# A subtraction moved from GpSimd to VectorE and behind another instruction, and norm steps moved within attention

## Chip, cores and metric

The kernel runs on one core of one Trainium2 chip. The metric is the device time of one execution in microseconds, the median of several runs. TensorE, VectorE, ScalarE, GpSimd and SyncE each work through a queue of their own in order and wait for one another through semaphores. In profile lines they are PE (PEld for its weight loads), DVE, ACT, POOL and SP; a DMA issued from a queue carries a q, as in SPq.

## The reference, cut to what matters

```python
# x: (8, 512, 32, 32) float32; C = 256, 4 heads of 64, N = 2 blocks
x = x + layer(_gn(x))                       # group norm over 16 channels x 1024 pixels, no affine part

def layer(x):
    t = silu(bn(conv1x1(x, cv1_w)))         # 512 -> 512 channels
    ys = [t[:, :C], t[:, C:]]
    for i in range(N):
        yi = ys[-1]
        z = silu(bn(conv3x3(yi, m_cv1_w[i])))
        q, k, v = conv1x1(z, m_qkv_w[i])    # 256 -> 3 x 256, split in 4 heads
        a = softmax(q^T (k + rw + rh) * 64**-0.5)   # 1024 x 1024 per head
        z = a v
        z = silu(bn(conv1x1(z, m_cv2_w[i])))
        ys.append(yi + z)
    return silu(bn(conv1x1(concat(ys), cv2_w)))     # 1024 -> 512 channels
```

## The kernel before

All data is float32. Images are taken in four pairs (`p` = 0 to 3; image a and image b). For each pair the kernel does, for block n = 0 and then n = 1: a 3x3 convolution of both images together, then for image a and then image b the q/k/v projection and attention, a 1x1 convolution, and the sum with the block's input. In between it does the final 1x1 convolution of the pair (`strassen`), and `cv1` with its group norm for the pair that comes next. The first pair is special in places: its n = 0 projections are direct ones, where all others use Strassen's scheme with seven products.

**The convolution** (`conv3x3`, L610) is Winograd's F(4,3). For each of two output channel blocks (`oc`) it works through i = 0, 1, 2, each with 48 TensorE products into two of three rotating PSUM buffers, and VectorE turns the products back into pixels: `c_t` (L672, L673; they read PSUM and a ScalarE copy `c_m`), `c_e` (L680), `c_r` (L687 to L690), then for i = 0 and 1 `c_k` (L693, L694), at i = 1 two row sets of `z` (L698 to L701) and at i = 2 the other two (L703, L704). ScalarE then applies SiLU in place on `z` (L495), one half image per instruction. For the last channel block at i = 2 the VectorE work is done in two parts (`parts`): first image a's, then image b's.

**The projection** (`project_strassen`, L903) takes `z` as four blocks: channel half times pixel half. It begins with w11 on block b11, then needs t1 = b12 - b11, both in channel block 0. t1 is made by `first_sum` (L897), which writes tile `t_z`. In the seven convolutions that are followed by a Strassen projection (n = 0 of p = 1, 2, 3 and n = 1 of all four) `first_sum` is called inside `conv3x3` at i = 1 of the last channel block (L697), on GpSimd; for image b it is called elsewhere on VectorE. Its products are `p_ps<-t_z,sq` (L916) and `p_ps<-sq,t_z` (L922). ScalarE copies the first products out of PSUM (`u_z`, `m_z`), and later products with z of channel block 1 are added onto the same PSUM buffers. t_z, the two position tables `r_in` (L942, loaded on SyncE's queue) and the kept products share one ring of six buffers (tag `pt`).

**Attention** (`attention_fast`, L1014) runs over four groups g (two heads, half of the queries), each in four steps of two 128-row key blocks. Step (g, at) issues its logits (L1037), ScalarE's exp (L1041), VectorE's accumulation of the denominators (L1055, L1057), and the products with v of the step before (L1071). Where g changes (a border) the finished PSUM buffer is evicted by a ScalarE copy (L1078) and a VectorE addition (L1079), and the next group's products with v wait for it, as there is one such buffer.

**Work behind attention's steps.** The dictionary `behind` hangs small pieces of other work on steps. Key (g, at) or g stands for the step whose v products have just been issued; the piece is queued on its engine behind the accumulation of the step after it. So key (0, 3) is the first border, (1, 3) the second, (2, 3) the third. `NORM_A` (L1964, image a, pairs 1 and 2) and `NORM_B` (L1965, image b, pairs 0 to 2) list the keys at which the generator `group_norm` (L792) for a coming image goes one step on: four statistics of one 128-channel block (L718, L719, VectorE), the mean over a group (`gm_ps`, a TensorE product, L725, and `dev` on VectorE), the reciprocal root (`gv_ps` on TensorE, then VectorE, then GpSimd L745, L802, L803), then the scaling on ScalarE (L809), four whole blocks in A, eight halves in B. In B two of the statistics are done before attention starts.

**What sets the order.** A scheduling layer lays out each engine's queue from the order of the code, a priority and its own idea of readiness; buffers of a ring are given out in the code's order. `tc.issue_after(ins)` puts all that is issued inside it behind `ins` on the same engine.

## Time and profile before

| | |
|---|---|
| runs | 2251.91, 2251.04, 2249.72 us; median 2251.04 |
| the profiled execution's own time | 2249.81 us |
| its span, first to last instruction | 2246.8 us |
| chain that ended last | PE 85%, DVE 11%, the rest 1% or less each |
| granted TensorE clock, mean | 0.999 |
| GpSimd `t_z` | 7 times, 1.28 us each, first at 364.9, last at 1986.4 |
| VectorE `t_z` at the same line (image b) | 7 times, 0.685 us each |
| end of the seven convolutions on TensorE | 372.5, 671.3, 923.0, 1219.6, 1471.0, 1767.3, 1994.0 us |

In a timeline each line is: start in us from the span's start, duration, engine, line and operation, tile written and tiles read, shapes, how often, and in brackets the idle time before it and who ended it. Instructions of VectorE overlap by some tenths of a microsecond, so what one costs the queue is the distance from its start to the next start. "n=1" below means the second block's convolution; the times of the list above alternate n=1, n=0 and so on, the first being n=1 of the first pair.

### The profile page before, as it was taken

To read this page: it belongs to the slowest core of one execution; us is meant where nothing else is said; L and a number is where in the kernel's file an instruction comes from. 1 tells how busy PE (TensorE), PEld (TensorE's weight loads), DVE (VectorE), ACT (ScalarE), POOL (GpSimd) and SP (SyncE) were. 2 spreads that over 40 slices of the span, in tenths; PEclk is the share of its full clock that TensorE was granted. 3 is DMA by queue.
4 is the path that set the end of the run, shared out by engine and by line. 5 is a ranking of instruction groups with operands and counts; after the bars stand their busy time and mean duration, and the time that the engine had idled before them with its cause. 6 is when DMAs were issued, how large, how long until landed. Compare 5 with 4: busy or idle time off the path is not lost.

```text
span 2246.8 us, 40264 instructions
## 1 busy us (share of the span) xinstructions
PE 2200.9 (98%) x16346; PEld 1080.6 (48%) x16346; DVE 1728.7 (77%) x2648; ACT 1099.6 (49%) x1332; POOL 224.4 (10%) x417
## 2 busy tenths in 40 slices
PE   7999999999999999999999999999999999999998
PEld 3653437343474444634447343654344734473443
DVE  7988879878678688877857868986794868797652
ACT  7554653644225665456324666455622455335533
POOL 4322210000220000000021000000012000000001
PEclk9999999999999999999999999999999999999999
DMA  9854447321581324511257141532136611350214
GB/s 273 308 163 150 150 151 261 109 78 45 140 275 49 118 81 145 183 58 67 67 159 261 30 169 35 197 116 77 58 76 173 233 39 34 102 198 30 67 50 112
DMA packets 134309, 285.60 MB, mean 127 GB/s; under 512 B 33540, under 2 KB 61184, under 8 KB 133092
## 3 DMA queue, kind: packets, MB, share of 16 engines
q1 hardware_dynamic: 102212, 197.34, 26.7%
q0 software_dynamic: 31904, 85.61, 13.3%
q8 instruction: 131, 2.15, 0.4%
q14 instruction: 62, 0.51, 0.1%
HBM read 214.86 MB, written 68.03 MB: 126 GB/s over the span
## 4 chain that ended last, share of the span: by engine, by line
PE 85%; DVE 11%; issue 1%; ACT 1%; DMA 1%; SPq 0%; POOL 0%; DVEq 0%; ACTq 0%; POOLq 0%
PE av_ps L1071 18%; PE l_ps L1037 18%; PE c L1305 9%; PE c_ps L653 7%; PE c_new L1305 6%; PE p_ps L916 6%; PE ps L523 5%; PE m_ps L1285 5%; PE x_ps L1405 4%; PE p_ps L922 3%; PE s_ps L1089 1%; DVE acc L1057 1%; DVE c_e L680 1%; PE p_ps L886 1%; DVE c_t L673 1%
## 5 line engine op out<-in xcount | busy, mean ns | idle before, releaser
L1041 ACT ACTIVATE pt<-l_ps 128x1024 f32<-128x1024 f32 x512 | 495.5, 1023 | 332.1 <-PE l_ps L1037 218.8
L1057 DVE TENSOR_TENSOR acc<-acc,pt 128x1024 f32<-128x1024 f32 x384 | 469.6, 1223 | 44.6 <-ACT pt L1041 16.2
L1071 PE MATMUL av_ps<-pt,vT 64*64 64x512 f32 x4096 | 484.8, 590 | 5.2 <-DVE z L1079 4.9
L1037 PE MATMUL l_ps<-q,kr 64*64 64x512 f32 x4096 | 486.3, 590 | 3.0 <-ACT pt L1041 1.9
L1071 PEld LDWEIGHTS av_ps<-pt,vT 64*64 64x64 f32 x4096 | 156.3, 133 | 284.8 <-issue 233.5
L1037 PEld LDWEIGHTS l_ps<-q,kr 64*64 64x64 f32 x4096 | 157.5, 133 | 273.2 <-issue 247.0
L653 PE MATMUL c_ps<-v_in,u 128*64 128x128 f32 x4320 | 239.1, 273 | 2.5 <-issue 2.5
L653 PEld LDWEIGHTS c_ps<-v_in,u 128*64 128x64 f32 x4320 | 235.8, 137 | 9.4 <-issue 9.4
L1285 PE MATMUL m_ps<-z,m_sb 128*128 128x512 f32 x256 | 114.1, 593 | 0.0
L658 ACT COPY c_m<-c_ps 128x512 f32<-128x512 f32 x48 | 28.0, 584 | 170.1 <-PE c_ps L653 140.8
L916 PE MATMUL p_ps<-t_z,sq 128*128 128x512 f32 x224 | 107.0, 595 | 0.0
L1079 DVE TENSOR_TENSOR z<-av_ps,z 128x512 f32<-128x512 f32 x64 | 44.1, 689 | 79.1 <-ACT z L1078 79.1
L1055 DVE TENSOR_TENSOR acc<-pt 128x1024 f32<-128x1024 f32 x64 | 78.0, 1219 | 18.0 <-PE s_ps L1089 11.2
L495 ACT ACTIVATE t<-m_ps,bh,sh 128x512 f32<-128x512 f32 x64 | 46.3, 773 | 91.2 <-PE m_ps L1285 91.2
L916 PE MATMUL p_ps<-z,sq 128*128 128x512 f32 x168 | 80.1, 604 | 5.3 <-ACT z L495 5.2
L1355 POOL DMA_DIRECT2D c_out<-in_x_dram x56 | 50.2, 954 | 293.2 <-ACT c_out L495 288.5
L1285 PEld LDWEIGHTS m_ps<-z,m_sb 128*128 128x128 f32 x256 | 47.8, 190 | 56.8 <-issue 52.5
L1147 DVE TENSOR_TENSOR z<-z,rs 128x512 f32<-128x512 f32 x64 | 42.3, 686 | 27.4 <-DMA rs<-r_dram 27.2
L495 ACT ACTIVATE c_out<-cz,bh,sh 128x512 f32<-128x512 f32 x14 | 16.8, 1301 | 89.1 <-DVE cz L1382 89.1
L495 ACT ACTIVATE z<-z,bh,sh 128x512 f32<-128x512 f32 x64 | 47.6, 804 | 25.8 <-DVE z L704 25.2
L1405 PE MATMUL x_ps<-t_x,sw 128*128 128x512 f32 x128 | 55.9, 592 | 0.0
L922 PEld LDWEIGHTS p_ps<-sq,z 128*128 128x128 f32 x336 | 42.7, 191 | 26.6 <-issue 12.7
(313 smaller groups left out, 3143.4 us busy)
## 6 DMA issues: line engine op xcount, KB each, us to landing
u<-u SPq DMA_DIRECT2D x135, 512.0 KB, 4.8
rs<-r_dram SPq DMA_DIRECT2D x126, 128.0 KB, 3.1
sq<-sq SPq DMA_DIRECT2D x42, 384.0 KB, 5.9
x<-in_x_dram SPq DMA_DIRECT2D x28, 512.0 KB, 7.0
r_in<-r SPq DMA_DIRECT2D x28, 512.0 KB, 4.9
y_in<-y SPq DMA_DIRECT2D x28, 512.0 KB, 4.4
c_out<-in_x_dram POOLq DMA_DIRECT2D x56, 256.0 KB, 5.1
out_dram<-c_out POOLq DMA_DIRECT2D x56, 256.0 KB, 3.3
```

What stands on the lines that cost most here:

```text
L495: silued[0] = nc.scalar.activation(dst, src, AF.Silu, scale=sh[:, k : k + 1], bias=bh[:, k : k + 1])
L523: last_product[0] = nc.tensor.matmul(ps[:, half, :], w_of(k), rhs_of(k, half), start=(k == begin), stop=(k == end))
L653: conv_product[0] = nc.tensor.matmul(to[o], us[cp][:, k, row, c, o], rhs, start=(k == 0), stop=(k == NM - 1),)
L916: nc.tensor.matmul(ps[:, o, :], w[:, o, :], rhs, start=not onto, stop=True, skip_group_check=onto)
L922: nc.tensor.matmul(v[:, ts(j, P)], rhs[:, ts(j, P)], w[:, 2, :], start=j == 0 and not onto, stop=True, skip_group_check=True,)
L1037: nc.tensor.matmul(ps[kh * HD : (kh + 1) * HD, hd, :], kr[r, c, o : o + HD], q[r, c, ts(half, HALF)], start=True, stop=True,)
L1041: last_exp[0] = exp = nc.scalar.activation(pt, ps, AF.Exp, scale=SCALE)
L1057: ins = nc.vector.tensor_tensor(accs[g], accs[g], pt[i], ALU.add)
L1071: nc.tensor.matmul(avs[g][hd * HD : (hd + 1) * HD, kh, :], vT[r, j, o : o + HD], pt[i][r, hd, :], start=(j == 0), stop=(j == NJ - 1),)
L1285: nc.tensor.matmul(pss[half][:, oc, :], m2_sb[:, n, k, ts(oc, P)], ao[:, k, ts(half, HALF)], start=(k == 0), stop=(k == NM - 1),)
L1305: nc.tensor.matmul(ps[:, o, :], w[:, k, ts(o, P)], rhs[part][:, c], start=(k == 0 and not onto), stop=(k == KB - 1), skip_group_check=onto,)
L1405: nc.tensor.matmul(ps[:, o, :], w[:, c, ts(o, P)], rhs[c], start=(c == 0 and not onto), stop=(c == 1), skip_group_check=onto,)
```

## The change

The call of `first_sum` in `conv3x3` moves from i = 1 to i = 2, and from GpSimd to VectorE: it is issued behind image a's last `z` instruction (L704, the new `placed`), ahead of image b's part. `first_sum` loses its engine argument. `NORM_A` has key 1 in place of (2, 3), and `NORM_B` has key 1 in place of (0, 1); as each key moves the same generator by one step, the steps between shift with it.

```diff
                         if i == 1:
-                            if oc == NM - 1 and summed is not None:
-                                t = first_sum(summed, nc.gpsimd)
                             stt(dst[:, 1], tiles(big_d), -0.5, tiles(d_), ALU.mult, ALU.add)
...
                         if final:
                             stt(dst[:, 0, tl], tiles(r0), -6.0, tiles(big_s[:, xs_]), ALU.mult, ALU.add)
-                            stt(dst[:, 3, tl], tiles(r1), -6.0, tiles(big_d[:, xs_]), ALU.mult, ALU.add)
+                            placed = stt(dst[:, 3, tl], tiles(r1), -6.0, tiles(big_d[:, xs_]), ALU.mult, ALU.add)
+                            if oc == NM - 1 and part == 0 and summed is not None:
+                                with tc.issue_after(placed.ins):
+                                    t = first_sum(summed)
...
-        def first_sum(z, engine=nc.vector):
+        def first_sum(z):
             t = act.tile([P, 2, HALF], F32, tag="pt", name="t_z", bufs=n_pt)
-            engine.tensor_tensor(t[:, 0], z[:, 0, ts(1, HALF)], z[:, 0, ts(0, HALF)], ALU.subtract)
+            nc.vector.tensor_tensor(t[:, 0], z[:, 0, ts(1, HALF)], z[:, 0, ts(0, HALF)], ALU.subtract)
...
-        NORM_A = ((0, 1), (0, 3), (1, 1), (1, 2), 2, (2, 1), (2, 2), (2, 3), 3, (3, 1))
-        NORM_B = ((0, 1), (0, 3), (1, 1), (1, 2), 2, (2, 1), (2, 2), (2, 3), 3, (3, 1), (3, 2), (3, 3))
+        NORM_A = ((0, 1), (0, 3), 1, (1, 1), (1, 2), 2, (2, 1), (2, 2), 3, (3, 1))
+        NORM_B = ((0, 3), 1, (1, 1), (1, 2), 2, (2, 1), (2, 2), (2, 3), 3, (3, 1), (3, 2), (3, 3))
```

In the changed program the queues stand so at each of the seven handovers. VectorE has t_z between image a's L704 and image b's L687. TensorE has the 128x128 products with z ahead of the products with t_z, where they stood behind the first of them. ScalarE has two SiLU instructions of image a, then `u_z`, two more, then `m_z`, where `u_z` and `m_z` stood ahead of all four. On SyncE's queue the two `r_in` loads stand behind later weight loads of the ring. In image a's attention of pairs 1 and 2 the `gm_ps` product stands one step ahead of the second border, where it stood behind it.

## The prediction

> **What bounds the kernel now.** I read the page's first part, then what TensorE waits for, then the timelines around one convolution's end and one attention.

> ```profile
> PE 2200.9 (98%) x16346; PEld 1080.6 (48%) x16346; DVE 1728.7 (77%) x2648; ACT 1099.6 (49%) x1332; POOL 224.4 (10%) x417
> ```

> ```profile
> PE p_ps L916 <- ACT z L495: 5.2, 6, 0.9
> PE av_ps L1071 <- DVE z L1079: 4.9, 5, 1.6
> ...
> PE p_ps L922 <- DVE c_t L673: 2.5, 4, 0.6
> ```

> (columns: total us, times, longest). TensorE is busy all but 45.9 us of the span, in one queue, in order. So a microsecond that TensorE waits anywhere is a microsecond of the span, unless a later wait shrinks by it, and later waits are few. The change can win at most the waits shown: 5.2 + 2.5 where seven convolutions hand over to the projection, and 4.6 of the 4.9 at borders that its norm steps touch (1.57 at 739.08 and 1287.38, 0.90 at 818.49, 0.55 at 1366.43).

> The handover, TensorE (start, duration, line):

> ```profile
> 372.47 1.98 PE L916 MATMUL p_ps<-z,sq 128*128 128x512 f32 x4
> 374.29 1.88 PE L916 MATMUL p_ps<-t_z,sq 128*128 128x512 f32 x4
> 376.80 1.13 PE L922 MATMUL p_ps<-sq,z 128*128 128x128 f32 x8 [0.63 <-DVE c_t L673]
> 377.76 1.06 PE L922 MATMUL p_ps<-sq,t_z 128*128 128x128 f32 x8
> 379.69 3.70 PE L916 MATMUL p_ps<-z,sq 128*128 128x512 f32 x8 [0.87 <-ACT z L495]
> ```

> VectorE and GpSimd at the same place:

> ```profile
> 364.70 0.69 DVE L680 SCALAR_TENSOR_TENSOR c_e<-c_ps,c_t 128x512 f32<-128x512 f32 x1
> 365.30 1.15 DVE L688 SCALAR_TENSOR_TENSOR c_r<-c_t 128x256 f32<-128x256 f32 x1
> ...
> 376.24 0.42 DVE L673 TENSOR_TENSOR c_t<-c_ps,c_m 128x256 f32<-128x256 f32 x1
> ...
> 378.37 0.42 DVE L704 SCALAR_TENSOR_TENSOR z<-c_r,c_k 128x256 f32<-128x256 f32 x1
> 378.71 0.28 DVE L687 SCALAR_TENSOR_TENSOR c_r<-c_t,c_e 128x128 f32<-128x128 f32 x1
> ```

> ```profile
> 364.89 1.28 POOL L900 TENSOR_TENSOR t_z<-z 128x512 f32<-128x512 f32 x1 [19.18 <-ACT z L495]
> ```

> VectorE runs without a gap from 365 to 382, behind TensorE. GpSimd's t_z (1.28 us) lies over it and L688 takes 1.15 in place of 0.42. But t_z is ready at 366.2, eight microseconds before TensorE reads it at 374.29.

> **Part 1, the difference on VectorE.** Removed: seven GpSimd t_z, and what they cost VectorE. By the start-to-start distances L688 lasts 1.08 where 0.33 is usual: 0.75 lost, in the four convolutions n=1 (372, 923, 1471, 1994). In n=0 of the second and third pair (671, 1219) L687 loses 1.71 - 0.33 = 1.38. In n=0 of the last pair (1767) nothing: the t_z of 1761.06 lies over L672 and L673, which read PSUM and keep their 0.68. Sum 4 x 0.75 + 2 x 1.38 = 5.8 us. [...]

> Added: a VectorE subtraction of 0.68 (0.60 start to start; the same line already runs seven times on VectorE with median 0.685), placed behind L704 of the first image's part in the changed program's order. That is late: TensorE's s1 products need t_z. The changed program also has TensorE's order moved: z products (1.82), then the four 128x128 z products (0.96), then t_z's. Worked out for the handover at 372.47: VectorE is 0.75 earlier, so L673 ends at 376.66 - 0.75 = 375.91, and the 128x128 products start 0.14 later at 376.05 (as 376.80 stood to 376.66) and are through at 377.0. L704 starts at 377.62, t_z at 377.96, ends 378.64; TensorE gets it at 378.76, a wait of 1.75. Then 1.81 for s1 on t_z, 0.96 for its 128x128 products: the next z products start at 381.53, where they started at 379.69. **+1.84 us**, four times.

> At 671.32: t_z runs 675.48 to 676.16, TensorE has it at 676.28, z products at 679.06 instead of 677.84: **+1.22**, twice. At 1767.31 nothing is won: L704 at 1771.15, t_z until 1772.17, z products at 1775.07 instead of 1772.83: **+2.24**, once. Sum 7.36 + 2.44 + 2.24 = **+12.0 us**. From 379.69 to the first logits at 393.10 TensorE has no idle, so the delay goes straight on.

> What else moves: ScalarE's u_z copy falls behind two of the first image's z activations and m_z behind all four. In the sum ScalarE does activations 378.07 to 379.6, u_z to 380.6, two more to 382.1, m_z to 383.1; TensorE wants u_z gone at 381.5 and m_z at 383.3. This just fits, 0.2 us spare: 0, or up to 0.5 a handover (+3.5). Not below 0. On SyncE's queue the two r_in loads fall behind up to six ring loads, the last of which waits for the convolution's last product: issue near 373.5 instead of 362.84, landing 3.5 to 6.0 (the page's table of DMA issues has 4.9), so by 379.6; VectorE's L946 asks for it at 383.42 + 1.8. Cost 0. On GpSimd's queue the stores behind t_z can only start earlier: 0.

> **Part 2, norm steps.** In the first image's attention (second and third pair of images) statistics three and four, the reciprocal root and the first two activations go one step earlier (a step is two 128-row blocks, some 3.43 us of TensorE), the second activation thereby off border three; the mean goes two steps earlier. In the second image's attention (first to third pair) statistic three goes two steps later, onto border one, and statistic four one step later, off it.

> ```profile
> 717.06 1.90 PE L1037 MATMUL l_ps<-q,kr 64*64 64x512 f32 x16
> ...
> 725.09 0.17 PE L725 MATMUL gm_ps<-mv,gmat 64*64 64x4 f32 x1
> ...
> 739.08 1.95 PE L1071 MATMUL av_ps<-pt,vT 64*64 64x512 f32 x16 [1.57 <-DVE z L1079]
> ```

> ```profile
> 719.53 1.28 DVE L718 BATCH_NORM_STATS2 st<-x 128x6 f32<-128x512 f32 x2
> 720.84 0.21 DVE L719 BATCH_NORM_AGGREGATE mv<-st 128x2 f32<-128x12 f32 x1
> ```

> gm_ps is a TensorE product in the same queue. It now stands 4.2 us behind its last statistic. In the changed order it stands two pairs of steps earlier, at 717.06, but its last statistic only one: VectorE needs from 711.87 one accumulation (1.13), statistics (1.31 and 0.13), two accumulations (2.42), statistics (1.31 and 0.21): 718.38. TensorE stands still until 718.5: +1.44. Later exp(2,3) is behind the moved activation, exp(3,0) and the border's copy end about 738.4, its VectorE half at 739.1, and the border's products start at 739.15 in place of 739.08. So what the border gives (1.1 to 1.2 of the 1.57, after the shift) the gm_ps wait takes: **+0.1**, twice.

> Second image: the border at 818.49 is met with 0.05 wait instead of 0.90, but gm_ps then stands at 822.85 with its statistic at 823.6: wait 0.9, net +0.1. At 1366.43: 0.55 won, 0.9 paid, **+0.4**. First pair (263): no border wait to win; statistic four and a u step end at 270.4 where gm_ps stood at 269.20, then gv_ps 274.6 for 273.20: **+1.4**. Sum of part 2: **+2.0 us**; its ends are -4.6 (all border waits gone, no new one) and +4.

> The new waits could cost more than their length: [...] The longest new wait is 1.8 us. The row nearest is the 1.57 us wait at 739.08, whose 16 products take 1.95 against 1.90 before. By the row 0[...]. I take 0 and leave it for the far tail.

> Together +12.0 + 2.0 = **+14.0 us** on the profiled execution: 2249.8 + 14.0 = 2263.8 (its span 2246.8, and 3.0 around it, unchanged). The median of the runs shown is 2251.04, 1.2 higher, within their spread of 2.2; I say 2264.

> **Rivals.** (A) The norm steps give what they cost before and gm_ps does not wait: +12.0 - 4.6 = +7.4, 2257. For it: the order of VectorE's queue is known, my start times of the statistics are not measured. Against: VectorE's queue is full there. (B) ScalarE is late: m_z misses its 0.2 us spare, +14 + 3.5, 2267. For it: seven activations and copies end to end; against: all durations are rows. (C) The other side: VectorE, not TensorE, sets the pace after the handover. Its last convolution instruction comes 0.15 earlier four times, 0.78 earlier twice, 0.60 later once: -1.6, and with the borders' -4.6 it is -6.2, 2243.6. It decides if TensorE has slack of 1.8 us between handover and attention. For it: VectorE runs 17 instructions into the attention (to 397.9). Against: VectorE idles there 1.08, 2.99 and 0.79 for ScalarE and TensorE, and TensorE never for it. (D) The subtraction isn't late at all: excluded, the changed order has it behind L704, and the products read it.

> **Chances.** My forecast (2260 to 2266) 0.65, A 0.12, B 0.13, C 0.05, rest (half clock, or waits absorbed to within noise) 0.05. Range 2256 to 2269 takes in A, B and the forecast. About 0.2%, 4.5 us, is what a measurement tells from no change. Slower 0.92, same 0.03, faster 0.05.

> **What would show it.** Right: TensorE's wait for DVE t_z of about 1.75 us before L917's t_z products in seven places (none for ScalarE's z any more), gm_ps waits near 1 us for L720 in five attentions, L688 back at 0.42. Wrong: z products less than 7.5 us behind a convolution's last product; or border waits gone without gm_ps waits (A); or waits for ScalarE u_z or m_z (B).

## The result and the profile after

The changed kernel's six runs have a median of 2266.12 us (2263.44 to 2268.74), those of the kernel before beside them 2250.76 us (2249.72 to 2253.74): ratio 1.0066, 95% interval 1.0053 to 1.0079. It is slower by 15.4 us. The execution that was profiled is its slowest, 2268.74 us with a span of 2267.4, against 2249.81 us for the profiled one of before.

Part 1 of the page, and below it TensorE's waits (total us, times, longest), both of the changed kernel:

```profile
PE 2209.2 (97%) x16346; PEld 1087.7 (48%) x16346; DVE 1727.0 (76%) x2655; ACT 1098.7 (48%) x1332; POOL 215.1 (9%) x410
```

```profile
PE gm_ps L726 <- DVE mv L720: 13.3, 6, 7.9
PE p_ps L917 <- DVE t_z L901: 10.6, 7, 1.5
PE p_ps L923 <- DVE c_t L673: 7.3, 7, 1.6
...
PE av_ps L1072 <- DVE z L1080: 0.3, 1, 0.3
```

The waits are where the sum put them: a new one for t_z at all seven handovers; c_t's grown from 2.5 us to 7.3; the one for ScalarE's z (5.2) gone; border waits from 4.9 to 0.3; and five new gm_ps waits (13.3 less the start's 7.9). But TensorE's busy time has also grown, by 8.3 us, with the same number of products. The sum had put nothing there. (Line numbers from L696 on differ by one or two from those of before.)

TensorE's timeline of the changed kernel at the first handover (n=1), and at the next (n=0, where c_t had been waited for only 0.28 us):

```profile
377.69 1.13 PE L923 MATMUL p_ps<-sq,z 128*128 128x128 f32 x8 [1.61 <-DVE c_t L673]
380.34 3.78 PE L917 MATMUL p_ps<-t_z,sq 128*128 128x512 f32 x4 [1.52 <-DVE t_z L901]
...
682.41 1.98 PE L917 MATMUL p_ps<-t_z,sq 128*128 128x512 f32 x4 [1.52 <-DVE t_z L901]
```

Four products on t_z take 1.98 us at 682.41 and 3.78 at 380.34. The busy times of one stretch name the reason (start:end and length; busy time and instructions of PE, PEld, DVE, ACT and POOL; granted TensorE clock; DMA share; GB/s):

```profile
380.30:385.00 4.70, 4.66 (x10) 2.60 (x11) 3.36 (x9) 4.10 (x6) 0.00 (x0) 0.50 0.07 27
```

TensorE came out of two idle stretches, 1.61 and 1.52 us with 1.1 us of work between, at half clock (0.50 granted), and the four products took 3.78 us in place of 1.98. In this execution that happened at 380, 936 and 1489, but not at 2017 after the very same two waits.

On VectorE the sum's picture holds:

```profile
366.93 0.41 DVE L688 SCALAR_TENSOR_TENSOR c_r<-c_t 128x256 f32<-128x256 f32 x1
...
379.60 0.69 DVE L901 TENSOR_TENSOR t_z<-z 128x512 f32<-128x512 f32 x1
```

L688 is back at 0.41 (1.15 before). t_z ends at 380.29, and TensorE starts on it 0.05 us later. VectorE's next instruction starts at 380.20: the overlap that start-to-start distances take off is 0.08 or 0.09 us here, not some tenths.

### The profile page after: what moved, and what is told of

It is laid out like the page before. It is cut to its first block, busy times and chain, and to the rows that moved or that the text cites. A ratio compares the mean times of both kernels' runs of the same rounds, so it can differ in the third digit from the quotient of the medians.

```text
span 2267.4 us, 40245 instructions
## 1 busy us (share of the span) xinstructions
PE 2209.2 (97%) x16346; PEld 1087.7 (48%) x16346; DVE 1727.0 (76%) x2655; ACT 1098.7 (48%) x1332; POOL 215.1 (9%) x410
## 4 chain that ended last, share of the span: by engine, by line
PE 85%; DVE 11%; issue 1%; ACT 1%; POOL 0%; DVEq 0%; ACTq 0%
PE av_ps L1072 18%; PE l_ps L1038 18%; PE c L1306 9%; PE p_ps L917 7%; PE c_ps L653 6%; PE c_new L1306 6%; PE ps L523 5%; PE m_ps L1286 5%; PE x_ps L1406 4%; PE p_ps L923 3%; PE s_ps L1090 1%; DVE acc L1058 1%; DVE c_e L680 1%; DVE c_t L673 1%; PE p_ps L887 1%
## 5 line engine op out<-in xcount | busy, mean ns | idle before, releaser
L917 PE MATMUL p_ps<-t_z,sq 128*128 128x512 f32 x224 | 111.6, 622 | 10.6 <-DVE t_z L901 10.6
L1056 DVE TENSOR_TENSOR acc<-pt 128x1024 f32<-128x1024 f32 x64 | 78.0, 1218 | 18.0 <-PE s_ps L1090 11.2
L495 ACT ACTIVATE t<-m_ps,bh,sh 128x512 f32<-128x512 f32 x64 | 46.3, 774 | 91.0 <-PE m_ps L1286 91.0
L917 PE MATMUL p_ps<-z,sq 128*128 128x512 f32 x168 | 81.0, 603 | 0.0
L495 ACT ACTIVATE z<-z,bh,sh 128x512 f32<-128x512 f32 x64 | 47.7, 805 | 59.5 <-DVE z L702 59.4
L917 PEld LDWEIGHTS p_ps<-t_z,sq 128*128 128x128 f32 x224 | 40.4, 198 | 46.8 <-issue 32.7
L495 ACT ACTIVATE c_out<-cz,bh,sh 128x512 f32<-128x512 f32 x14 | 16.8, 1306 | 89.6 <-DVE cz L1383 89.6
```

The lines of the kernel that those rows point to most:

```text
L495: silued[0] = nc.scalar.activation(dst, src, AF.Silu, scale=sh[:, k : k + 1], bias=bh[:, k : k + 1])
L917: nc.tensor.matmul(ps[:, o, :], w[:, o, :], rhs, start=not onto, stop=True, skip_group_check=onto)
```

## The experiments

Twelve kernels ran. Each time is beside runs of the kernel before on the same chip.

| run | median us | before us | ratio, 95% interval |
|---|---|---|---|
| e1, t_z alone | 2266.02 | 2251.52 | 1.0064 (1.0050 to 1.0078) |
| e2, norm steps alone | 2253.09 | 2251.52 | 1.0005 (0.9997 to 1.0014) |
| e3, t_z on VectorE, early | 2248.52 | 2251.52 | 0.9987 (0.9980 to 0.9993) |
| e4, changed, first wait filled | 2260.74 | 2251.52 | 1.0043 (1.0029 to 1.0057) |
| e5, changed, t_z after the second part | 2286.80 | 2250.15 | 1.0163 (1.0148 to 1.0179) |
| e6, norm steps, later mean | 2252.22 | 2250.15 | 1.0009 (1.0000 to 1.0017) |
| e7, e3 with e6 | 2249.49 | 2250.15 | 0.9994 (0.9986 to 1.0003) |
| e8, changed, one wait for two | 2270.43 | 2250.15 | 1.0087 (1.0074 to 1.0101) |
| e9, steps off the borders | 2254.58 | 2251.16 | 1.0015 (1.0008 to 1.0022) |
| e10, e3 with e9 | 2250.78 | 2251.16 | 0.9996 (0.9987 to 1.0004) |
| e11, e3, with A of e9 and B of e6 | 2245.20 | 2250.68 | 0.9975 (0.9965 to 0.9985) |
| e12, A of e9 and B of e6 | 2247.52 | 2250.68 | 0.9987 (0.9980 to 0.9994) |

A second measure is finer than these medians. TensorE's queue is nearly full, so the distance between the same two products in two profiles compares one stage without what differs elsewhere. The handover stage at n=1 runs from the first z products to the next image's, the A stage from the n=0 handover to the next image's (so it holds the n=0 handover and, in pairs 1 and 2, the attention with A's steps), the B stage from there to the next convolution's end.

| stage, us | before | changed | e1 | e3 | e4 | e6 | e9 | e11 |
|---|---|---|---|---|---|---|---|---|
| n=1 handover, pair 0 | 76.89 | 81.44 | 78.43 | 76.64 | 78.44 | 76.88 | 76.89 | 76.64 |
| pair 1 | 76.90 | 80.04 | 78.44 | 76.64 | 78.44 | 76.89 | 76.90 | 76.64 |
| pair 2 | 76.89 | 80.07 | 80.01 | 76.64 | 78.43 | 76.88 | 76.89 | 76.64 |
| pair 3 | 76.89 | 78.44 | 80.12 | 76.64 | 78.43 | 76.88 | 76.89 | 76.64 |
| A stage, pair 1 | 110.43 | 111.22 | 111.35 | 109.54 | 111.22 | 111.10 | 109.25 | 108.43 |
| pair 2 | 110.44 | 111.22 | 111.34 | 109.81 | 111.22 | 111.43 | 109.39 | 108.70 |
| n=0 handover, pair 3 | 75.18 | 77.10 | 77.11 | 75.31 | 77.11 | 75.68 | 76.41 | 75.31 |
| B stage, pair 1 | 141.27 | 141.24 | 141.27 | 140.92 | 141.25 | 140.48 | 142.66 | 140.50 |
| pair 2 | 140.92 | 142.16 | 141.52 | 141.68 | 141.25 | 140.49 | 144.06 | 140.51 |

**e1: the difference on VectorE alone.** The changed kernel with both norm tables as before:

```diff
-NORM_A = ((0, 1), (0, 3), 1, (1, 1), (1, 2), 2, (2, 1), (2, 2), 3, (3, 1))
-NORM_B = ((0, 3), 1, (1, 1), (1, 2), 2, (2, 1), (2, 2), (2, 3), 3, (3, 1), (3, 2), (3, 3))
+NORM_A = ((0, 1), (0, 3), (1, 1), (1, 2), 2, (2, 1), (2, 2), (2, 3), 3, (3, 1))
+NORM_B = ((0, 1), (0, 3), (1, 1), (1, 2), 2, (2, 1), (2, 2), (2, 3), 3, (3, 1), (3, 2), (3, 3))
```

> The difference on VectorE behind the first image's last part, norm steps left where they were. Theory (TensorE's in-order queue stands still for the late t_z): +12 us from the waits (about 1.6 us for c_t and 1.5 for t_z at the four convolutions n=1, 0.3 and 1.5 at the three n=0), and 0 to 7 more where TensorE comes out of the two waits at half clock: 2262 to 2269 us, border waits of 4.9 us still there, no gm_ps wait beyond the start's 8.0. Rival (the norm steps make most of the loss): under +5 us, below 2256.

Measured +14.5 us: this part is nearly all of the loss. TensorE's timeline of e1 at the first and the third n=1 handover:

```profile
380.33 1.98 PE L917 MATMUL p_ps<-t_z,sq 128*128 128x512 f32 x4 [1.52 <-DVE t_z L901]
...
1484.45 3.55 PE L917 MATMUL p_ps<-t_z,sq 128*128 128x512 f32 x4 [1.52 <-DVE t_z L901]
```

The waits are those of the changed kernel to a hundredth; here two of the four handovers fall to half clock, and not the same ones. The table separates the two costs: without half clock a handover is 78.43 - 76.89 = 1.54 us longer, with it 3.1 or more: the clock adds 1.6 to 1.7, and 3.0 at the changed kernel's first (81.44 - 78.43). The runs' spread of 5.8 us (2262.95 to 2268.75) is wide beside the 1.8 of e4, which has no half clock at its handovers.

**e2: the norm steps alone.** The kernel before with the changed tables.

> Only the norm steps moved, t_z as before on GpSimd. Theory: the border waits (4.9 us) go to 0.3, and five gm_ps waits of 0.9 to 1.4 us and 0.2 of gv_ps take their place: +2 us, 2252 to 2254 us, clock 0.999. Rival 1 (moving them off the borders wins what the borders cost): -4.6 us, 2246. Rival 2 (they carry the loss): +10 us or more.

Measured +1.6 us, interval -0.7 to +3.2: the theory's +2 fits, and neither rival does. By the run alone it can't be told from no change.

**e3: the same engine, the old place.** In the kernel before, at i = 1:

```diff
-t = first_sum(summed, nc.gpsimd)
+t = first_sum(summed)
```

with `first_sum` on VectorE.

> t_z on VectorE, but issued where GpSimd's was, before the second image's differences; norm steps as before. Theory (the place costs, not the engine): TensorE's order as before, no wait for t_z; VectorE gains the blocked 0.75 or 1.38 us and spends 0.6: -0.15 at four handovers, -0.78 at two, +0.60 at one: -1.6 us, 2248 to 2251. Rival (the seven added instructions on a busy VectorE are themselves the cost): +4 us or more, 2255, with longer c_t waits.

Measured -3.0 us, interval -4.5 to -1.6, a little more than expected. TensorE's timeline of e3:

```profile
377.62 1.13 PE L922 MATMUL p_ps<-sq,z 128*128 128x128 f32 x8 [0.37 <-DVE c_t L673]
```

t_z is there in time (TensorE reads it from 375.37 on, without a wait), and c_t is waited for 0.37 us where it was 0.63. Each n=1 handover is 0.25 us shorter than before. So on VectorE the seven instructions cost less than what GpSimd's had held up there; what costs is the late place.

**e4: fill the first wait.** The changed kernel, in the first image's projection:

```diff
 to_qk(ps_a, w["11"], b11)
+if table:
+    to_qk(ps_a, w["11"], b11)
```

The same four products are done again, over the first ones.

> The changed kernel with TensorE's first products of the projection (4 of 128x512 on z, 1.8 us) issued twice, the second overwriting the first, so that TensorE works through what was its wait for c_t; in the first image's projection only. Theory (half clock after two idle stretches close together): the t_z products take 1.98 us at all seven handovers, where three of the changed kernel's took 3.6 to 3.8; the wait for t_z stays 1.4 to 1.5 at the four n=1 and goes to 0 at the three n=0; all runs within 2 us, 2263 to 2265, at or below the fastest of the changed kernel's runs (2263.44). Rival (the slow products have another cause[...]): 3.6 to 3.8 us stay, 2266 to 2269 or more.

TensorE's timeline of e4, where the doubled products run until 378.4, then the stretch behind it:

```profile
378.39 1.13 PE L923 MATMUL p_ps<-sq,z 128*128 128x128 f32 x8
381.04 1.98 PE L917 MATMUL p_ps<-t_z,sq 128*128 128x512 f32 x4 [1.52 <-DVE t_z L901]
```

```profile
381.00:385.70 4.70, 4.66 (x17) 2.71 (x18) 3.35 (x9) 4.70 (x8) 0.00 (x0) 1.00 0.15 45
```

The wait for t_z is as long as ever, and t_z ends no earlier, but with TensorE at work in the other gap the granted clock is 1.00 in this stretch, and the products on t_z take 1.98 or 1.99 us at all seven handovers. Useless products on the bounding engine make the kernel 5.4 us faster than the changed one (2260.74 for 2266.12; 6.1 us when each is set against its own runs of the kernel before). So in these runs the half clock goes with TensorE's own idleness, not with t_z or its readers. e4 also leaves the waits by themselves: +9.2 us, interval +6.5 to +12.8, less than the 2263 to 2265 us expected, and with an interval that holds the 11.2 us which the stages give below.

**e5: the wait, longer.** The changed kernel with `part == 0` made `part == parts - 1`: t_z behind the second part.

> The changed kernel with t_z behind the first image's second and last part instead of behind its first. In the changed trace these are seven VectorE starts and 2.2 us later (379.60 to 381.81). Theory (TensorE waits in order for t_z): the wait grows from 1.52 to about 3.7 us at each of the seven handovers, +15 us over the changed kernel, and with 3.7 us of idle in one piece most of the seven come out at half clock (1.7 to 3 us each, against two to three of the changed kernel's): 2281 to 2295 us. Rival (some later wait shrinks by what this one grows): under +5, below 2271.

Measured 2286.80, in the range. The wait is 3.12 us, not 3.7 (t_z itself no longer stands ahead of the second part, 0.6 us that the expectation overlooked). TensorE's timeline of e5 at the first handover:

```profile
382.34 3.78 PE L917 MATMUL p_ps<-t_z,sq 128*128 128x512 f32 x4 [3.12 <-DVE t_z L901]
```

7 x 1.6 = 11.2 us of the 20.7 over the changed kernel is wait; the rest goes with half clock, which now meets six of seven handovers, two of the n=0 ones among them (the third, at 1243.33, does its products in 1.98 us after the same wait). No later wait takes the delay up.

**e8: one wait in place of two.** The changed kernel with the accumulators swapped between PSUM pools (`ps_b` from `big()`, `ps_v` from the attention pool).

> The changed kernel with the first two projection accumulators swapped between the two PSUM pools (p_ps of the t_z products in the large pool, that of the 128x128 products in the attention pool), so that the two waits of 1.6 and 1.5 us before the t_z products should come as one of about 3 us, t_z's own time unchanged. Theory 1 (half clock follows from idle in one piece): three or four of the four n=1 handovers at half clock, 2266 to 2270 us. Theory 2 (it follows from the idle share of some stretch of time): as often as in the changed kernel, half of them on average, 2263 to 2268. If the t_z products ran slow for a reason at t_z itself (its read of z beside ScalarE's activations), they stay as in the changed kernel, too.

TensorE's timeline of e8, two n=1 handovers:

```profile
380.13 3.38 PE L917 MATMUL p_ps<-t_z,sq 128*128 128x512 f32 x4 [3.45 <-DVE t_z L901]
...
934.48 1.96 PE L917 MATMUL p_ps<-t_z,sq 128*128 128x512 f32 x4 [3.45 <-DVE t_z L901]
```

3.45 us of idle in one piece were followed by half clock at two of four handovers of this profile (four products in 3.38 us here and in 3.17 at 1484.92, against 1.96 at the other two), which is the fastest of its five runs (2262.67 us, mean granted clock 0.997). The other four, 2266.53 to 2272.35 us, have a mean of 0.993 to 0.996, which speaks for more half clock in them. The same wait has either outcome: its length alone does not decide it. The last section has what the changed kernel's profile shows of it.

**e6 and e7: keep the border gain, move the mean.**

```diff
-NORM_A = ((0, 1), (0, 3), (1, 1), (1, 2), 2, (2, 1), (2, 2), (2, 3), 3, (3, 1))
-NORM_B = ((0, 1), (0, 3), (1, 1), (1, 2), 2, (2, 1), (2, 2), (2, 3), 3, (3, 1), (3, 2), (3, 3))
+NORM_A = ((0, 1), (0, 3), 1, (1, 1), (1, 3), 2, (2, 1), (2, 2), 3, (3, 1))
+NORM_B = ((0, 3), 1, (1, 2), (1, 3), 2, (2, 1), (2, 2), (2, 3), 3, (3, 1), (3, 2), (3, 3))
```

Both edit the kernel before; e7 has e3's t_z as well.

> The kernel before with the norm steps moved as in the change, but the mean one key later than the change has it (A: from (1,2) to (1,3); B: mean from (1,1) to (1,2) and root from (1,2) to (1,3)), one TensorE step of about 3.4 us, longer than the waits of 0.88 to 1.30. Theory (the border gain is real, and the early mean took it): gm_ps waits gone but for the start's 8.0, border waits near 0.3: -4 to -5 us, 2246 to 2248. Rival (moving the steps off the borders wins nothing, another wait takes their place): 2251 to 2253.

> t_z on VectorE at its old early place together with the norm steps with the later mean. Theory (the two gains lie at different places on TensorE's queue and add): -3 (measured for the early t_z alone) and -4 to -5: 2243 to 2245 us, below both kernels. Rival (they share one slack): 2246 to 2249.

Neither gain came: e6 +2.1 us, in its rival's range, and e7 wins 0.7 where e3 alone won 3.0, 0.5 us above its rival's range (each against the runs of before beside it). The wait that came in e6, among TensorE's waits, and VectorE behind A's mean:

```profile
PE gv_ps L725 <- DVE dev L737: 4.0, 4, 1.2
```

```profile
727.65 0.15 DVE L735 TENSOR_TENSOR dev<-mv,gm 128x4 f32<-128x4 f32 x1
727.84 1.23 DVE L1057 TENSOR_TENSOR acc<-acc,pt 128x1024 f32<-128x1024 f32 x1
728.98 0.15 DVE L736 TENSOR_TENSOR dev<-dev 128x4 f32<-128x4 f32 x1
```

The mean no longer waits (gm_ps is back at the start's 7.9) and the borders don't (0.3), but in VectorE's queue the small instructions that follow the mean now stand between accumulations of 1.2 us, so `dev` is late for the gv_ps product: 4.0 us in four waits where it was 1.2 in two. By the stage table the loss is in A alone (+0.7 and +1.0 us); B got shorter (-0.8 and -0.4). In A the waits only balance (1.57 us at the border before; 1.22 for gv_ps and 0.28 for `s_ps` now). What makes it longer is TensorE's busy time, 108.95 us for 108.00 in pair 2 with the same 710 products: logits and v products stand there one to ten at a time where they stood in sixteens. That this order is the cause is not shown.

**e9 and e10: off the borders, TensorE's order untouched.**

```diff
-NORM_A = ((0, 1), (0, 3), (1, 1), (1, 2), 2, (2, 1), (2, 2), (2, 3), 3, (3, 1))
-NORM_B = ((0, 1), (0, 3), (1, 1), (1, 2), 2, (2, 1), (2, 2), (2, 3), 3, (3, 1), (3, 2), (3, 3))
+NORM_A = ((0, 1), (0, 3), (1, 1), (1, 2), 2, (2, 1), (2, 2), 3, (3, 1), (3, 2))
+NORM_B = ((0, 1), (0, 2), (1, 1), (1, 2), 2, (2, 1), (2, 2), (2, 3), 3, (3, 1), (3, 2), (3, 3))
```

These too edit the kernel before; e10 has e3's t_z as well.

> The kernel before with two norm steps of each attention off the borders but mean and root products where they were: A: second to fourth activation one key later (from (2,3), 3, (3,1) to 3, (3,1), (3,2)); B: statistic four from (0,3) to (0,2). TensorE's order is that of before. Theory (a border wait can be won if no TensorE product of the norm is moved closer to its input): av_ps waits from 4.9 to 0.3, gm_ps and gv_ps waits as before, -4.6 us, 2245 to 2247. Rival (each border wait that goes comes back at another wait, as with the change's and the later mean's steps): 2250 to 2252.

> The same norm steps with t_z on VectorE at its early place. Theory (both gains add): -3.0 (early t_z alone, measured) and -4.6: 2242 to 2244 us, faster than both kernels. Rival (no gain at the borders): 2247 to 2249.

Both missed (+3.4 us, and -0.4 where -7 or more was expected). The stage table again divides them: A is 1.2 and 1.05 us shorter, B 1.4 and 3.1 longer. VectorE in e9 at B's border, then TensorE there and at the same place of the next pair:

```profile
819.23 0.21 DVE L719 BATCH_NORM_AGGREGATE mv<-st 128x2 f32<-128x12 f32 x1
819.36 0.64 DVE L1079 TENSOR_TENSOR z<-av_ps,z 128x512 f32<-128x512 f32 x1
```

```profile
820.05 1.95 PE L1071 MATMUL av_ps<-pt,vT 64*64 64x512 f32 x16 [2.29 <-DVE z L1079]
...
1368.11 3.53 PE L1071 MATMUL av_ps<-pt,vT 64*64 64x512 f32 x16 [1.94 <-DVE z L1079]
```

One key earlier put the statistic (1.28 us from 817.92, and the row shown) directly ahead of the border's eviction on VectorE, and the second of these waits, 1.94 us, was followed by half clock (3.53).

**e11 and e12: each attention its own fit.** NORM_A from e9, NORM_B from e6; e11 with e3's t_z as well.

> t_z on VectorE at its early place, A's activations one key later (as in the run with the steps off the borders, where that attention was 1.1 to 1.2 us shorter in each of two), B's statistics as in the change with the mean one key later (that attention was 0.4 to 1.2 us shorter). Theory (each attention has its own fit, and these two gains are real): 2 x 1.1 + 2 x 0.8 = 3.8 us below the early t_z alone (2248.5), 2244 to 2246 us. Rival (what was read in single profiles is noise, or comes back later): 2248 to 2250.

> The same norm steps with t_z left on GpSimd. Theory: about 3.4 us below the kernel before (2 x 1.15 in A, 0.8 and 0.4 in B), 2247 to 2249. Rival: no gain, 2250 to 2252.

Both came out in the expected ranges: e12 -3.2 us, e11 -5.5 us (interval -7.9 to -3.4), faster than both kernels. In e11's waits gm_ps has only the start's 7.8 us, gv_ps 1.6, the borders 1.5 and c_t 1.5.

## Why the prediction was right, and where its sum was not

The time was right, 2266.12 for 2264, and so was the mechanism: TensorE waits, in order, for a t_z that comes late. That the sum came out so near is luck, as errors of opposite sign met.

**TensorE's queue as the bound: held.** With the waits 1.6 us longer at seven places (e5) nothing absorbed them.

**Part 1, +12.0: right in kind, about 2 us too high.** The waits were as forecast. The profile's 1.61 and 1.52 us count from the end of the product before (372.47 + 1.98), the sum's 1.76 and 1.75 from when the next one could have started (372.47 + 1.82 or so); counted like the profile, the sum had 1.60 and 1.58. By e1's stages the handovers cost 4 x 1.54, 0.92 + 0.90 and 1.93, together 9.9 us, each 0.3 below its forecast (1.84, 1.22, 2.24). (The last, pair 3's n=0, may be less still: with t_z on GpSimd that stage took 75.18 in the profile of before, but 75.68 in e6 and 76.41 in e9, so GpSimd's t_z cost the profile of before little there.) Of the 0.3, some 0.1 is at the handover (the z products came 1.73 us late, 383.04 - 374.09 against 379.69 - 372.47, not 1.84). The rest came back between there and the first logits: 396.27 - 383.04 = 13.23 us in e1, 13.41 before. The later products stand in another order there and are through 0.18 us sooner, and the sum had carried the delay straight on.

**What GpSimd's t_z cost VectorE: as the rows said.** L688 went back from 1.15 us to 0.41. In e3 the wait for c_t shrank by 0.26 us with a further 0.60 of VectorE work ahead of it, so by that estimate GpSimd's t_z had cost some 0.86: nearer to the 0.75 of the rows than to its own whole 1.28.

**ScalarE and SyncE at 0: held.** No TensorE wait for u_z or m_z appears at the handovers (rival B), and the one for kr, which r_in feeds, is the 0.5 us of before.

**Part 2, +2.0 (its terms add up to 2.1): right in kind, 0.7 too high.** The gm_ps waits were 1.30, 1.30, 0.88, 0.88 and 1.08 us, against 1.44 twice, 0.9 twice and about 1.2. Against e1 or before, A's stages are 0.1 shorter and B's -0.02 and +0.33 (by e4, whose pair 2 has no chance gap); with the first pair's 1.08 and a gv_ps wait of 0.16 the sum is +1.3. Rival A, a border gain without gm_ps waits, fell with these waits.

**Half clock, set to 0: the step that failed.** The prediction took the row of one 1.57 us wait, followed by 16 products in 1.95 us (1.90 before), and left half clock for the far tail. The row was the wrong neighbour: it is one wait of 1.57, the handover has 1.61 + 1.52 within 4.3 us. Measured: half clock in three of four n=1 handovers of the changed profile (1.6, 1.6 and 3.0 us, 6.2 in all) and two of four in e1 (3.3 us); none with the gap filled (e4). At n=0, where the waits were 0.28 + 1.52 us, it never came (0 of 6 in these two profiles). Over the six runs of the changed kernel the mean granted clock sorts the times: 0.998 in the two of 2263.44 and 2263.49 us, 0.996 at 2265.01, 0.995 in the three of 2267.23 to 2268.74. Of the median's loss it is some 3 to 6 us: 2.7 above those two fastest runs, 4.2 as 15.4 less the 11.2 of waits, 6.1 as 15.4 less e4's 9.2. So two waits, each about as long as the row's single one, brought half clock at five of eight n=1 handovers of these two profiles.

So -2.1 in part 1, -0.7 in part 2 and the remainder, +4.2, put down to the clock: 14.0 became 15.4. The profiled execution (+18.9 us) had more than its share: besides 6.2 us of half clock, one issue gap of 0.86 us in pair 2's B stage, and chance at the start.

**Rival C, VectorE as the pace-setter: excluded** by e5, where VectorE has no more to do than in the changed kernel, only in another order, and 20.7 us more are lost. Its -6.2 us is near what e11 wins (-5.5), but on TensorE's queue, by waits removed, and with t_z early.

## What to carry to other kernels

When one engine's queue bounds the kernel, a small producer must be placed by when that queue reaches its reader: the same subtraction gains 3 us early and loses 14.5 late, on the same engine. A wait on TensorE costs its length and perhaps as much again in clock (1.6 to 3.0 us for waits of 3.1 here), and waits close together, here 1.61 and 1.52 us with 1.1 us of work between, must be added up before they are compared with a row that shows a single one. A step taken off one wait has to be followed to the next instruction in the queue that it lands in front of: three of the four ways to clear the borders tried here (the change, e6, e9) lost at another wait or in the other attention what they won or more, and a table of stage lengths found which half of e6 and of e9 was good.

## What the hardware showed

```profile
376.26:379.67 3.41, 1.13 (x8) 0.97 (x8) 3.41 (x13) 0.00 (x0) 0.00 (x0) 1.00 0.97 342
379.68:383.09 3.41, 2.75 (x4) 1.20 (x5) 3.38 (x11) 3.37 (x5) 0.00 (x0) 0.50 0.25 100
383.09:386.50 3.41, 3.41 (x12) 2.38 (x11) 0.60 (x2) 2.12 (x4) 0.00 (x0) 0.50 0.00 0
386.51:389.92 3.41, 3.41 (x15) 2.02 (x14) 0.69 (x1) 1.20 (x3) 0.00 (x0) 1.00 0.49 154
...
2011.25:2014.66 3.41, 1.80 (x5) 0.53 (x4) 3.41 (x10) 0.00 (x0) 0.00 (x0) 1.00 0.96 259
2014.67:2018.08 3.41, 1.89 (x10) 1.29 (x11) 3.38 (x14) 1.51 (x3) 0.00 (x0) 1.00 0.85 309
```

At the first handover one stretch holds 2.28 us of the two waits, and the two after it, busy for 2.75 and 3.41 us, are at half clock: these are the 3.0 us. At the last, a stretch ends between the same two waits, the two hold 1.61 and 1.52 us, and the clock stays at 1.00. An estimate from these numbers: a stretch of 3.41 us holds 1.61 us or more of 1.61 + 1.52 with 1.1 of work between in 0.64 of its possible positions, and 2.22 or more in 0.28. Half clock came at five of the eight n=1 handovers of the changed kernel and e1. In e4 a handover has one wait, of 1.52 us (n=1) or 0.32 (n=0). What happens between 1.61 and 2.22 us of idle, and whether idle time in such a stretch is what the clock follows, these two profiles do not show.

At the start, too, the length of a wait alone does not decide. At about 76 us TensorE waits for `v_in` (L607), for 2.22 us in the changed kernel and 2.87 in e3. TensorE's timeline of the changed kernel there, then that of e3:

```profile
75.49 5.38 PE L653 MATMUL c_ps<-v_in,u_new 128*64 128x128 f32 x64 [2.22 <-DVE v_in L607]
```

```profile
76.12 3.71 PE L653 MATMUL c_ps<-v_in,u_new 128*64 128x128 f32 x64 [2.87 <-DVE v_in L607]
```

64 products take 3.71 us in e3 and 5.38 in the changed kernel, whose granted clock is 0.50 from 75.89 to 79.30. The changed kernel's 2.22 us of idle lay in one stretch, from 72.47 to 75.88; e3's longer wait was followed by full speed. What half clock costs depends on what follows, too: e3, without it here, waits for the next v_in for 1.06 us at 83.01 and 1.61 at 101.49, the changed kernel, with it, only for 1.22 at 100.86. From the start of the 64 products to the end of the last of these waits it is 25.37 us in both, so the 1.7 us come back. At the handovers no later wait gave it back.
